# Four graph layers on one core: linear scores by one projection, the update gate from the reset gate's sum, a precomputed second hop, tanh for sigmoid, roots on GpSimd

## Chip, cores, metric

One core of a Trainium2 chip. Times are device microseconds of one execution. PE is TensorE (matmul), PEld its weight loads, DVE is VectorE, ACT is ScalarE, POOL is GpSimd. All executions quoted are in the fast state; repeats of one kernel agree within about 0.3%, once 0.4%.

## The reference, cut to what matters

x is [64, 256, 128] in fp32, adj is [256, 256]. Four layers, each added to its input after a layernorm and a relu:

```python
# layer 0, five steps                      # in_matrix = out_matrix = adj
u3 = h @ u3_w.T + u3_b
z = sigmoid(av @ w3_w.T + w3_b + u3)
r = sigmoid(av @ w4_w.T + w4_b + u3)
hv = tanh(av @ w5_w.T + w5_b + (r * h @ u5_w.T + u5_b))
h = (1.0 - z) * h + z * hv
# layer 1: hops x1 = A x0 and 2 A x1 - x0, concatenated, @ Theta1 + bias, relu
# layer 2: ((adj + I) h) W + bias, rows divided by their norm
# layer 3
pre = s1[:, :, None, :] + s2[:, None, :, :] + b_lin          # [b, i, j, 256]
h = where(pre >= 0, pre, 0.2 * pre)
attn = softmax(einsum('bije,e->bij', h, a) + adj, axis=2)
out = sigmoid(attn @ x)
```

## The kernel before

The batches go through in 32 pairs. Layer 3's scores are most of the work. For each row i of the 256, a relu of s2 plus row i's scalar is made on VectorE (two of three tiles) or ScalarE (every third), and TensorE reduces it over its 128 partitions with a stationary operand 32 columns wide. Four such matmuls use the four column groups of the array:

```python
for r in range(32):                       # one slot: rows r, 32+r, 64+r, 96+r of a row block
    for k in range(NE):                   # NE = 2 tiles a slot
        rl = relu_pool.tile([P, 4, NB, N], F32, name="rl")
        ...                               # 8 relus of 128x256, on VectorE or on ScalarE
        # four column groups of the array, which run side by side
        for g in range(4):
            nc.tensor.matmul(flat[g * 32:(g + 1) * 32, :], win[:, k, 31 - r:63 - r],
                             rl[:, g].rearrange("p b n -> p (b n)"), start=False, ...)
    background()                          # one stage of the next pair's layers 0 to 3, one of a softmax
```

I call the four matmuls of a tile a **quad**. The background of a gate step:

```python
pr = project([(w4t, mT), (u3t, hT)], "pr")       # two 128x512 products into one PSUM bank
pz = project([(w3t, mT), (u3t, hT)], "pz")
nc.scalar.activation(r, pr, AF.Sigmoid, bias=br, scale=1.0)
nc.scalar.activation(z, pz, AF.Sigmoid, bias=bz, scale=1.0)
nc.vector.tensor_mul(rh, r, hT)
yield
pv = project([(w5t, mT), (u5t, rh)], "pv")
```

The layernorm takes its root on ScalarE (`Sqrt`) and its reciprocal on VectorE. When the kernel is built, the framework's scheduler fixes the order of the instructions on each engine.

## Time and profile before

| | before |
|---|---|
| time | 7427.95 us, median of 3 (7426.46 to 7433.29) |
| TensorE busy | 7242 us (98%), ends modelled |
| VectorE busy | 6814 us (92%) |
| ScalarE busy | 5601 us (75%), of it 366 us of table loads |
| GpSimd busy | 0.7 us |

The prediction shows the main lines. One more view belongs beside it: the chain of work that ended last, in order of time, over one gate step of the kernel before. Columns: start in us, length in us, engine, tile, line, and the records. An fp32 matmul shows as two records.

```profile
3147.80 1.72 PE pz L212 x4
3149.51 1.85 PE pe L421 x16
3151.37 1.91 PE pv L212 x4
3153.28 3.57 PE pe L421 x32
3156.85 0.59 PE pt L197 x4
3157.44 1.85 PE pe L421 x16
3159.29 1.92 PE pm L205 x8
```

### The profile page before, as it was taken

Reading aid. Unit: us, or ns where it says so; the run is one execution under the profiler, and the core shown is the slowest. Engines: PE = TensorE matmul, PEld = TensorE weight load, DVE = VectorE, ACT = ScalarE, POOL = GpSimd, SP = SyncE. Lnnn points to the kernel's source line nnn. Section 1 sums busy time; section 2 is a strip of 40 time slices with the busy share of each in tenths; the row PEclk is TensorE's granted clock in tenths of the full one; section 3 lists DMA queues with packets and bytes.
Section 4 is the critical chain, followed back from the end, with each engine's and each line's share of the span. In section 5 each row is a group of like instructions: output and inputs, shape, how many; then the busy total and the mean of one; then the engine's idle time right before and its main releaser. Section 6 shows DMA issues by size and latency. Waiting matters only on the chain.

```text
span 7427.2 us, 120750 instructions
## 1 busy us (share of the span) xinstructions
PE 7242.1 (98%) x40713; PEld 2490.1 (34%) x40713; DVE 6813.8 (92%) x25298; ACT 5601.2 (75%) x12837; POOL 0.7 (0%) x6
## 2 busy tenths in 40 slices
PE   6999999999999999999999999999999999999999
PEld 3333333333333333333333333333333333333333
DVE  4998999999999999998999999999989999999999
ACT  3777777778777777777777777777877777777777
POOL 0000000000000000000000000000000000000000
PEclk8999999999999999999999999999999999999999
DMA  0000000000000000000000000000000000000000
GB/s 13 3 4 4 3 2 3 4 4 3 2 4 3 4 3 2 4 3 4 4 3 3 3 4 4 3 2 4 3 4 3 2 4 3 4 2 2 2 2 3
DMA packets 38816, 25.83 MB, mean 3 GB/s; under 512 B 3504, under 2 KB 38192, under 8 KB 38192
## 3 DMA queue, kind: packets, MB, share of 16 engines
q1 hardware_dynamic: 35088, 17.05, 0.8%
q8 instruction: 319, 5.23, 0.3%
q14 instruction: 305, 2.50, 0.1%
q10 hardware_dynamic: 3104, 1.05, 0.1%
HBM read 9.70 MB, written 8.39 MB: 2 GB/s over the span
## 4 chain that ended last, share of the span: by engine, by line
PE 87%; DVE 12%; ACT 1%; issue 0%; DMA 0%; SPq 0%; ACTq 0%; DVEq 0%
PE pe L421 58%; PE pm L205 7%; DVE rl L417 6%; PE pr L212 4%; PE pz L212 4%; PE pv L212 4%; PE pe L403 2%; PE pe L399 2%; PE pt L197 2%; DVE h L180 1%; PE po L222 1%; PE po L381 1%; PE pa L212 1%; PE pb L212 1%; DVE stats L173 1%; PE pt L189 1%
## 5 line engine op out<-in xcount | busy, mean ns | idle before, releaser
L417 DVE TENSOR_SCALAR rl<-s,s 128x256 f32<-128x256 f32 x21848 | 5868.7, 347 | 46.8 <-PE pe L421 44.5
L421 PE MATMUL pe<-rl,win 128*32 128x512 f32 x32768 | 5102.9, 599 | 93.4 <-DVE rl L417 93.4
L415 ACT ACTIVATE rl<-s,s 128x256 f32<-128x256 f32 x10920 | 4531.2, 497 | 399.6 <-PE pe L421 394.5
L421 PEld LDWEIGHTS pe<-rl,win 128*32 128x32 f32 x32768 | 1295.7, 109 | 3162.2 <-DVE rl L417 1569.0
L205 PE MATMUL pm<-adj_t,h 128*128 128x256 f32 x1280 | 336.0, 400 | 2.8 <-ACT h L274 2.8
L258 DVE TENSOR_TENSOR rh<-r,hT 128x512 f32<-128x512 f32 x160 | 109.8, 686 | 237.9 <-ACT r L254 237.3
L205 PEld LDWEIGHTS pm<-adj_t,h 128*128 128x128 f32 x1280 | 232.4, 195 | 166.3 <-issue 78.0
L249 ACT COPY mT<-pm 128x512 f32<-128x512 f32 x160 | 93.7, 586 | 155.3 <-PE pm L205 154.3
L254 ACT ACTIVATE r<-pr,gate_b 128x512 f32<-128x512 f32 x160 | 109.9, 687 | 114.5 <-PE pr L212 114.5
L369 ACT ACTIVATE sc<-sc,nmx 128x256 f32<-128x256 f32 x128 | 64.5, 504 | 157.3 <-DVE nmx L365 156.8
L212 PE MATMUL pr<-mT,w4t 128*128 128x512 f32 x320 | 178.9, 641 | 3.5 <-ACT mT L249 3.5
L212 PE MATMUL pv<-mT,w5t 128*128 128x512 f32 x320 | 179.5, 643 | 0.0
L403 PE MATMUL pe<-a_lin,s 128*128 128x256 f32 x512 | 168.6, 419 | 0.0
L212 PE MATMUL pr<-hT,u3t 128*128 128x512 f32 x320 | 167.3, 604 | 0.0
L212 PE MATMUL pz<-mT,w3t 128*128 128x512 f32 x320 | 165.9, 600 | 0.0
L212 PE MATMUL pv<-rh,u5t 128*128 128x512 f32 x320 | 164.5, 595 | 0.0
L262 ACT ACTIVATE hv<-pv,gate_b 128x512 f32<-128x512 f32 x160 | 108.7, 680 | 73.1 <-PE pv L212 73.0
L212 PE MATMUL pz<-hT,u3t 128*128 128x512 f32 x320 | 163.4, 592 | 0.0
L256 ACT ACTIVATE z<-pz,gate_b 128x512 f32<-128x512 f32 x160 | 109.3, 683 | 64.8 <-PE pz L212 64.8
L265 DVE TENSOR_TENSOR hv<-hv,hT 128x512 f32<-128x512 f32 x160 | 109.7, 686 | 37.7 <-ACT hv L262 36.3
L403 PEld LDWEIGHTS pe<-a_lin,s 128*128 128x128 f32 x512 | 80.9, 188 | 181.4 <-issue 179.8
L399 PE MATMUL pe<-s,a_lin 128*128 128x512 f32 x256 | 141.1, 640 | 0.0
(108 smaller groups left out, 3577.9 us busy)
## 6 DMA issues: line engine op xcount, KB each, us to landing
xin<-in_x_dram SPq DMA_DIRECT2D x64, 128.0 KB, 2.2
out_dram<-o SPq DMA_DIRECT2D x64, 128.0 KB, 1.8
w_raw<-in_L_gnn_w_w_dram ACTq DMA_DIRECT2D x3, 128.0 KB, 2.6
th_raw<-in_L_gnn_Theta_dram ACTq DMA_DIRECT2D x1, 320.0 KB, 3.4
adj_n<-in_adj_dram SPq DMA_DIRECT2D x1, 256.0 KB, 4.7
w_raw<-in_L_gnn_u_w_dram ACTq DMA_DIRECT2D x2, 64.0 KB, 2.6
bias<-in_L_gnn_bias_dram ACTq DMA_DIRECT2D x2, 64.0 KB, 3.5
w<-in_L_gnn_weight_dram ACTq DMA_DIRECT2D x1, 64.0 KB, 3.1
```

What stands on the lines that cost most here:

```text
L197: nc.tensor.transpose(pt[:, b, c, :], ht[:, b, c * P:(c + 1) * P], ident)
L205: nc.tensor.matmul(pm[:, b, :], h[:, b, c, :], a[:, c, :], start=(c == 0), stop=(c == NC - 1))
L212: nc.tensor.matmul(pp.rearrange("p b n -> p (b n)"), w, t.rearrange("p b n -> p (b n)"), start=(k == 0), stop=(k == len(pairs) - 1))
L254: nc.scalar.activation(r, pr, AF.Sigmoid, bias=br, scale=1.0)
L256: nc.scalar.activation(z, pz, AF.Sigmoid, bias=bz, scale=1.0)
L258: nc.vector.tensor_mul(rh, r, hT)
L265: nc.vector.tensor_sub(hv, hv, hT)
L399: nc.tensor.matmul(flat, a_lin[:, k, :P], s2[k].rearrange("p b n -> p (b n)"), start=(k == 0), stop=False, skip_group_check=True)
L403: nc.tensor.matmul(pe[:, b, :], s1[k][:, b, ic * P:(ic + 1) * P], a_lin[:, k, :], start=False, stop=False, skip_group_check=True)
L415: nc.scalar.activation(rl[:, g, b, :], s2[k][:, b, :], AF.Relu, bias=sc, scale=1.0)
L417: nc.vector.tensor_scalar(rl[:, g, b, :], s2[k][:, b, :], sc, 0.0, op0=OP.add, op1=OP.max)
L421: nc.tensor.matmul(flat[g * 32:(g + 1) * 32, :], win[:, k, 31 - r:63 - r], rl[:, g].rearrange("p b n -> p (b n)"), start=False, stop=(r == ...
```

## The change

It aims to take work off TensorE and ScalarE. Row i's own part of the linear scores is constant along j and cancels in the softmax; the other part is one projection of the layer's input. The update gate's sum is the reset gate's sum plus a difference of weights, so its product is added to the same PSUM bank after the reset gate has been read. The second hop uses a precomputed 2AA. Sigmoid becomes 0.5 + 0.5 tanh(x/2), and roots become a power on GpSimd, so that ScalarE needs one table. The core of the diff, with cuts marked:

```diff
+        nc.gpsimd.tensor_scalar(var, mv[:, :, 1], LN_EPS, None, op0=OP.add)
+        nc.gpsimd.tensor_tensor(rstd, var, neg_half, op=OP.pow)
-        nc.scalar.activation(std, mv[:, :, 1], AF.Sqrt, bias=eps_t, scale=1.0)
-        nc.vector.reciprocal(rstd, std)
 ...
             pr = project([(w4t, mT), (u3t, hT)], "pr")
-            pz = project([(w3t, mT), (u3t, hT)], "pz")
-            nc.scalar.activation(r, pr, AF.Sigmoid, bias=br, scale=1.0)
+            nc.scalar.activation(r, pr, AF.Tanh, bias=br, scale=0.5)
+            nc.tensor.matmul(pr.rearrange("p b n -> p (b n)"), w34t, mT.rearrange("p b n -> p (b n)"),
+                             start=False, stop=True, skip_group_check=True)
-            nc.scalar.activation(z, pz, AF.Sigmoid, bias=bz, scale=1.0)
+            nc.scalar.activation(z, pr, AF.Tanh, bias=bz, scale=0.5)
 ...
-        pt = to_token(c1T, "pt")
-        c1 = tok("c1")
-        nc.scalar.copy(c1, pt)
-        yield
-        pm = mix_nodes(c1, adj_n, "pm")
+        pm = mix_nodes(h, adj_2, "pm")
 ...  (y: four additions of the bias become one with a broadcast operand)
         norm_relu(x3, h3)
+        nc.gpsimd.tensor_scalar(x3, x3, 0.5, None, op0=OP.add)
 ...
-            for k in range(NE):
-                nc.tensor.matmul(flat, a_lin[:, k, :P], s2[k]..., start=(k == 0), ...)
-            for b in range(NB):
-                for k in range(NE):
-                    nc.tensor.matmul(pe[:, b, :], s1[k][:, b, ...], a_lin[:, k, :], ...)
+            nc.tensor.matmul(flat, lin_w, hT.rearrange("p b n -> p (b n)"), start=True, ...)
```

More of the change, by code (lines that the diff above doesn't have):

```diff
@@ L88 @@
     make_identity(nc, ident)
-    eps_t = const.tile([P, 1], F32, name="eps_t")
-    nc.vector.memset(eps_t, LN_EPS)
+    neg_half = const.tile([P, NB * NC], F32, name="neg_half")
+    nc.vector.memset(neg_half, -0.5)
     adj_n = const.tile([P, NC, N], F32, name="adj_n")
@@ L118, in load_transposed @@
         return t
-    w3t = load_transposed(w3_w, "w3t")
     u3t = load_transposed(u3_w, "u3t")
     w4t = load_transposed(w4_w, "w4t")
+    w34t = load_transposed(w3_w, "w34t")
+    nc.vector.tensor_sub(w34t, w34t, w4t)
     w5t = load_transposed(w5_w, "w5t")
     u5t = load_transposed(u5_w, "u5t")
+    nc.vector.tensor_scalar(u5t, u5t, 0.5, None, op0=OP.mult)
+    adj_2 = const.tile([P, NC, N], F32, name="adj_2")
+    for c in range(NC):
+        pq = bank([P, N], "pq")
+        for k in range(NC):
+            nc.tensor.matmul(pq, adj_t[:, k, c * P:(c + 1) * P], adj_n[:, k, :], start=(k == 0), stop=(k == NC - 1))
+        nc.vector.tensor_scalar(adj_2[:, c, :], pq, 2.0, None, op0=OP.mult)
     braw = const.tile([P, 5], F32, name="braw")
@@ L132 @@
     nc.vector.tensor_add(gate_b[:, 2:3], braw[:, 2:3], braw[:, 4:5])
+    nc.vector.tensor_scalar(gate_b[:, 0:2], gate_b[:, 0:2], 0.5, None, op0=OP.mult)
     bz, br, bh = gate_b[:, 0:1], gate_b[:, 1:2], gate_b[:, 2:3]
@@ L137 @@
     th = const.tile([P, 3, D], F32, name="th")
-    nc.vector.tensor_copy(th[:, 0, :], th_raw[:, 0, :])
     nc.vector.tensor_add(th[:, 1:3, :], th_raw[:, 1:3, :], th_raw[:, 3:5, :])
+    nc.vector.tensor_sub(th[:, 0, :], th_raw[:, 0, :], th[:, 2, :])
     w2 = const.tile([P, D], F32, name="w2")
@@ L158 @@
     nc.vector.memset(win, 0.0)
-    a_lin = const.tile([P, NE, N], F32, name="a_lin")
+    a_lin = const.tile([P, NE, P], F32, name="a_lin")
     nc.vector.memset(a_lin, ALPHA)
@@ L163 @@
         nc.vector.tensor_scalar(a_lin[:, k, :], a_lin[:, k, :], acol[:, k:k + 1], None, op0=OP.mult)
+    pl = bank([P, P], "pl")
+    for k in range(NE):
+        nc.tensor.matmul(pl, adj_n[:, k, P:2 * P], a_lin[:, k, :], start=(k == 0), stop=(k == NE - 1))
+    lin_w = const.tile([P, P], F32, name="lin_w")
+    nc.vector.tensor_copy(lin_w, pl)
     def norm_relu(src, h):
@@ L174, in norm_relu @@
             nc.vector.bn_aggr(mv[:, k, :], stats[:, k, :])
-        std = work.tile([P, NB * NC], F32, name="std")
-        nc.scalar.activation(std, mv[:, :, 1], AF.Sqrt, bias=eps_t, scale=1.0)
+        var = work.tile([P, NB * NC], F32, name="var")
+        nc.gpsimd.tensor_scalar(var, mv[:, :, 1], LN_EPS, None, op0=OP.add)
         rstd = work.tile([P, NB * NC], F32, name="rstd")
-        nc.vector.reciprocal(rstd, std)
+        nc.gpsimd.tensor_tensor(rstd, var, neg_half, op=OP.pow)
         for k in range(NB * NC):
@@ L251, in front @@
             pr = project([(w4t, mT), (u3t, hT)], "pr")
-            pz = project([(w3t, mT), (u3t, hT)], "pz")
             r = feat("r")
-            nc.scalar.activation(r, pr, AF.Sigmoid, bias=br, scale=1.0)
+            nc.scalar.activation(r, pr, AF.Tanh, bias=br, scale=0.5)
+            nc.tensor.matmul(pr.rearrange("p b n -> p (b n)"), w34t, mT.rearrange("p b n -> p (b n)"),
+                             start=False, stop=True, skip_group_check=True)
             z = feat("z")
-            nc.scalar.activation(z, pz, AF.Sigmoid, bias=bz, scale=1.0)
+            nc.scalar.activation(z, pr, AF.Tanh, bias=bz, scale=0.5)
             rh = feat("rh")
-            nc.vector.tensor_mul(rh, r, hT)
+            nc.vector.scalar_tensor_tensor(rh, r, 1.0, hT, op0=OP.add, op1=OP.mult)
             yield
@@ L265, in front @@
             nc.vector.tensor_sub(hv, hv, hT)
-            nc.vector.tensor_mul(hv, hv, z)
+            nc.vector.scalar_tensor_tensor(hv, z, 1.0, hv, op0=OP.add, op1=OP.mult)
             hT_new = feat("hT")
-            nc.vector.tensor_add(hT_new, hT, hv)
+            nc.vector.scalar_tensor_tensor(hT_new, hv, 0.5, hT, op0=OP.mult, op1=OP.add)
             hT = hT_new
@@ L291, in front @@
         yield
-        pt = to_token(c1T, "pt")
-        c1 = tok("c1")
-        nc.scalar.copy(c1, pt)
-        yield
-        pm = mix_nodes(c1, adj_n, "pm")
+        pm = mix_nodes(h, adj_2, "pm")
         c2T = feat("c2T")
-        nc.vector.scalar_tensor_tensor(c2T, pm, 2.0, hT, op0=OP.mult, op1=OP.subtract)
+        nc.scalar.copy(c2T, pm)
         yield
@@ L301, in front @@
         y = tok("y")
-        for k in range(NB * NC):
-            b, c = divmod(k, NC)
-            nc.vector.tensor_add(y[:, b, c, :], po[:, b, c, :], bias1)
+        nc.vector.tensor_add(y.rearrange("p b c d -> p (b c) d"), po.rearrange("p b c d -> p (b c) d"),
+                             bias1.unsqueeze(1).to_broadcast([P, NB * NC, D]))
         x2 = tok("x2")
@@ L318, in front @@
         y = tok("y")
-        for k in range(NB * NC):
-            b, c = divmod(k, NC)
-            nc.vector.tensor_add(y[:, b, c, :], po[:, b, c, :], bias2)
+        nc.vector.tensor_add(y.rearrange("p b c d -> p (b c) d"), po.rearrange("p b c d -> p (b c) d"),
+                             bias2.unsqueeze(1).to_broadcast([P, NB * NC, D]))
         yield
@@ L327, in front @@
         nc.vector.tensor_scalar(nrm, nrm, NORM_EPS * NORM_EPS, None, op0=OP.max)
-        nc.scalar.activation(nrm, nrm, AF.Sqrt)
         rn = work.tile([P, NB, NC], F32, name="rn")
-        nc.vector.reciprocal(rn, nrm)
+        nc.gpsimd.tensor_tensor(rn.rearrange("p b c -> p (b c)"), nrm.rearrange("p b c -> p (b c)"), neg_half,
+                                op=OP.pow)
         x3 = tok("x3", bufs=3)
@@ L340, in front @@
         norm_relu(x3, h3)
+        nc.gpsimd.tensor_scalar(x3, x3, 0.5, None, op0=OP.add)
         yield
         pt = to_feature(h3, "pt")
-        hT = feat("hT")
+        hT = feat("hT3")
         nc.scalar.copy(hT, pt)
@@ L356, in front, with tail @@
             yield
-        READY[p] = (x3, h3, s1, s2)
-    def tail(p, ic, pe, x3, h3):
+        READY[p] = (x3, h3, hT, s1, s2)
+    def tail(p, ic, pe, xh, h3):
         t = work.tile([P, NB, N], F32, name="sc")
@@ L372, in tail @@
         nc.vector.reciprocal(rs, sums)
+        nc.vector.tensor_scalar(rs, rs, 0.5, None, op0=OP.mult)
         yield
@@ L384, in tail @@
         for b in range(NB):
-            nc.scalar.activation(o[:, b, :], po[:, b, :], AF.Sigmoid, scale=rs[:, b:b + 1])
-        nc.vector.tensor_add(o, o, x3[:, :, ic, :])
+            nc.scalar.activation(o[:, b, :], po[:, b, :], AF.Tanh, scale=rs[:, b:b + 1])
+        nc.vector.scalar_tensor_tensor(o, o, 0.5, xh[:, :, ic, :], op0=OP.mult, op1=OP.add)
         nc.sync.dma_start(out[p * NB:(p + 1) * NB, ic * P:(ic + 1) * P, :].rearrange("b p d -> p b d"), o)
@@ L392, in scores @@
     def scores(p, background):
-        x3, h3, s1, s2 = READY.pop(p)
+        x3, h3, hT, s1, s2 = READY.pop(p)
         for ic in range(NC):
@@ L397, in scores @@
             flat = pe.rearrange("p b n -> p (b n)")
-            for k in range(NE):
-                nc.tensor.matmul(flat, a_lin[:, k, :P], s2[k].rearrange("p b n -> p (b n)"),
-                                 start=(k == 0), stop=False, skip_group_check=True)
-            for b in range(NB):
-                for k in range(NE):
-                    nc.tensor.matmul(pe[:, b, :], s1[k][:, b, ic * P:(ic + 1) * P], a_lin[:, k, :],
-                                     start=False, stop=False, skip_group_check=True)
+            nc.tensor.matmul(flat, lin_w, hT.rearrange("p b n -> p (b n)"),
+                             start=True, stop=False, skip_group_check=True)
             for r in range(32):
```

## The prediction

> **What bounds the kernel now.** I read the page's parts 1 and 2 first, then its chain, its costliest groups, the waits, and last a table of busy time by stretch over one pair of batches. Busy shares and chain of the kernel before:
>
> ```profile
> PE 7242.1 (98%) x40713; PEld 2490.1 (34%) x40713; DVE 6813.8 (92%) x25298; ACT 5601.2 (75%) x12837; POOL 0.7 (0%) x6
> PE 87%; DVE 12%; ACT 1%; issue 0%; DMA 0%; SPq 0%; ACTq 0%; DVEq 0%
> L417 DVE TENSOR_SCALAR rl<-s,s 128x256 f32<-128x256 f32 x21848 | 5868.7, 347 | 46.8 <-PE pe L421 44.5
> L421 PE MATMUL pe<-rl,win 128*32 128x512 f32 x32768 | 5102.9, 599 | 93.4 <-DVE rl L417 93.4
> L415 ACT ACTIVATE rl<-s,s 128x256 f32<-128x256 f32 x10920 | 4531.2, 497 | 399.6 <-PE pe L421 394.5
> ```
>
> At first sight TensorE is the bound (98%, 87% of the chain). That is too simple, since matmul ends are modelled. In the chain, sixteen score matmuls take 1.85 us when TensorE is pressed, so the two tiles of one slot of 4 rows cost it 1.85 us. VectorE issues one relu in 0.264 us (69 in a row took 18.20 us in the timeline): with 2 of 3 tiles of 8 relus each, a slot costs it 2 x 2/3 x 8 x 0.264 = 2.81 us. So a slot without other work is VectorE's, and TensorE binds only where layers 0 to 3 of the next pair lie beside the scores. Two chain pieces (start, length, what) and one pair cut into stretches (PE, PEld, DVE, ACT, POOL busy) show this:
>
> ```profile
> 3057.22 53.43 PE pe L421 x326
> ...
> 3128.78 1.72 PE pr L212 x4
> 3130.50 1.72 PE pz L212 x4
> 3132.22 1.85 PE pe L421 x16
> ```
>
> ```profile
> 3110.00:3128.00 18.00, 18.00 (x78) 6.11 (x74) 15.60 (x64) 11.80 (x26) 0.00 (x0) 1.00 0.01 1
> 3128.00:3208.00 80.00, 80.00 (x483) 28.77 (x482) 75.48 (x261) 67.11 (x153) 0.00 (x0) 1.00 0.01 3
> 3208.00:3277.00 69.00, 65.26 (x374) 23.05 (x370) 64.72 (x252) 50.72 (x117) 0.00 (x0) 1.00 0.02 7
> 3277.00:3342.00 65.00, 65.00 (x370) 20.92 (x370) 65.00 (x253) 50.56 (x120) 0.00 (x0) 1.00 0.00 1
> ```
>
> A: tail of the pair before and start of the front (18 us). B: the five gate steps, 17.2 us each (80 us). C: layers 1 to 3 (69 us). D: scores alone (65 us). In A and B TensorE is full: a gate step's pieces in the chain, 5 x 1.85 + 1.93 (mix) + 1.92 + 1.72 + 1.91 (projections) + 0.6 (transposes), sum to 17.3. But VectorE has 15.6 + 75.5 = 91.1 of those 98 us. C is a chain of VectorE work (norms, y, x) with waits. D is VectorE's alone: it is busy 65.00 of 65, and the 53.43 us piece gives 1.31 us per tile where TensorE could do 0.93. **VectorE is the floor everywhere, TensorE lies 7% above it in 98 us of a pair.** What VectorE idles is, in the waits (total, times, longest):
>
> ```profile
> DVE rh L258 <- ACT r L254: 237.3, 51, 10.6
> DVE s L350 <- PE pa L212: 60.9, 54, 2.3
> DVE c2T L298 <- PE pm L205: 59.1, 21, 11.0
> DVE y L321 <- PE po L222: 50.2, 32, 5.5
> ```
>
> Of 7427 - 6814 = 613 us idle, the first front, which nothing overlaps, has some 100 (it ends near 133 us; its five rh waits alone are 45). About 500 us are left, 16 per pair. One pair takes (7427 - 137) / 32 = 228 us.
>
> **What the Trainium skill says.** "Trainium Kernel Development and Optimization", its opening words on reading a trace: matmul busy time is a bad metric, because matmuls are pipelined. The trace agrees: score matmuls last 599 ns but sixteen pass in 1.85 us. "ScalarE: Activation LUTs", sections "What ACT_TABLE_LOAD costs" and "Table sets": a switch of set is a 1283 ns load; exp and tanh share a set, sqrt and sigmoid sit in others. The trace agrees: loads of 1283 ns, 94 + 94 + 54 + 31 + 12 = 285 of them, 365.7 us. "SBUF — State Buffer", section "Who interferes with whom": a VectorE instruction that uses both its ports holds a port pair shared with GpSimd, and the other is blocked for the whole instruction. The relus move 256 elements in 264 ns; at the 0.96 GHz that "VectorE: DVE Perf Modes", section "Specifications", gives, one element a cycle would need 267 ns and any overhead on top, so they must run in a two-element mode and hold that pair. GpSimd does nothing in this trace (0.7 us), so no run here shows the collision yet.
>
> **The change part by part** (per pair; 32 pairs).
> 1. Linear scores. Per row block, out: two 128x512 products and four 128x256 ones; in: one 128x512. In the chain at 3110 us the old ones are 1.06 + 1.06 + 0.43 + 0.63 + 1.06 = 4.24 us, the new one 1.06: 3.2 us less for each of two blocks. One block's lie in A, where TensorE is full; the other's around 3045 to 3057, where VectorE was busy without a gap: hidden. Busy time: 141.1 + 168.6 less about 70 = 239 us.
> 2. Update gate. Two products become one that accumulates on the reset gate's sum: one product of two records less per step, 0.86 us in the chain (1.72 for four), 4.3 us per pair, all in B (163 us busy).
> 3. Hop. Four transposes (21.5 us over the run) and one copy go; the other copy moves c2T from VectorE (0.69) to ScalarE. One stage less in the front.
> 4. Tanh, power. All 285 loads but the first go: 366 us of ScalarE, plus 38 + 7 us of roots. ScalarE is never full (80 us of B hold 67), so I count almost nothing. VectorE loses its reciprocals, 4 x 0.17 + 0.17 = 0.86.
> 5. Broadcast bias: 0.88 becomes about 0.68, twice: 0.4. New on VectorE: two small scalings, 2 x 0.15 = 0.3. The fused forms of the gate arithmetic cost as the plain ones (691 against 686 ns).
> 6. GpSimd gets 9 small instructions for roots and one 128x512 addition.
>
> On the path: A + B lose 4.3 + 3.2 = 7.5 us of TensorE, but VectorE's 91.1 us stop the gain at 6.9; with two nearly full engines I expect 4.5. C loses 0.69 + 0.86 + 0.4 - 0.3 = 1.65 us of VectorE work and perhaps 1.3 of its 4.3 us idle: 3. D gains nothing. GpSimd takes back an estimated 2.5: ten instructions, each a hand-over that stops VectorE for about 0.25 us, taken from the trace's only GpSimd work (100 to 292 ns apiece). Sum 4.5 + 3 - 2.5 = 5.0 us; x 31 = 155, plus 7 in the first front (shorter hop, no loads): 162. **7428 - 162 = about 7265 us**, 2.2% less.
>
> **The rivals.** (a) Everything removed pays: 424 us of TensorE (239 + 163 + 22) make 7000. For it: TensorE's 87% of the chain. Against: D is VectorE's, and VectorE alone needs 6814 - 60 plus the first front's idle 100, about 6850. (b) GpSimd becomes the wait. Norm and root stand in the middle of VectorE's stream; before, only 8.6 us were lost to the root, because some seven relus were put between. If GpSimd is locked out by those very relus and starts only when VectorE stops, each of 128 norms exposes about 2 us and each of 32 roots 1.5: 300 us, which gives 7428 - 162 - 80 (the 2.5 already taken) + 300, about 7490. Nothing in the profile of before speaks against it. (c) TensorE must wait for the reset gate to be read before it adds the difference: 0.69 us of ScalarE plus hand-over, about 0.9, as much as the saved 0.86. Score matmuls put between would hide it; if they don't, B gains nothing and about 5 x 0.86 x 0.6 = 2.6 us per pair are lost again: 7345. (d) The rh wait has another cause than TensorE's load; then 3 us per pair stay: about 7360.
>
> **Range and chances.** Centre 7265; (a) half true pulls to 7080, (b) half true with (c) pushes to 7430. The 2% line is 7279, so faster and same are nearly even: 0.50 faster, 0.43 same, 0.07 slower.
>
> **What would show each step.** Table loads 285 to a few, and ScalarE near 5200 us with no gain of its own; VectorE's busy time near 6750 and still at 93%; TensorE below VectorE's share or its score matmuls now waiting for relus in B; a gate step below 17.2 us, not below 16.5; D's slots unchanged at 2.81 us; the rh wait per pair about halved. Wrong would be shown by a wait of h on GpSimd's rstd over 1 us each (b), by relus longer than 264 ns apart beside GpSimd work, or by TensorE idle before the difference product (c).

## The result, and the profile after

8363.73 us median (8362.24 to 8364.41) against 7428.31: ratio 1.126, 95% interval 1.1244 to 1.1276. The change is 12.6% slower. (A ratio is the mean time of one kernel's fast runs over that of the other's of the same rounds, so not quite the ratio of the quoted medians.)

Busy times, chain by engine, and the two groups of the score work, after:

```profile
PE 7986.9 (96%) x39637; PEld 2439.2 (29%) x39637; DVE 6825.9 (82%) x24984; ACT 5189.8 (62%) x12393; POOL 284.4 (3%) x326
PE 77%; DVE 19%; POOL 3%; issue 1%; ACT 0%; DMA 0%; ACTq 0%; SPq 0%; DVEq 0%
L434 PE MATMUL pe<-rl,win 128*32 128x512 f32 x32768 | 6068.1, 604 | 287.5 <-DVE rl L430 286.7
L430 DVE TENSOR_SCALAR rl<-s,s 128x256 f32<-128x256 f32 x21848 | 5878.9, 345 | 11.1 <-PE pe L434 9.8
```

TensorE has 1076 records fewer and is busy 745 us longer. The score matmuls are the same 32768 records with nearly the same mean duration (604 against 599 ns), yet together they occupy 6068 us instead of 5103, 965 us more. Records that used to lie beside each other no longer do. The chain over the same part of a gate step shows how:

```profile
3014.43 1.00 PE pe L434 x8
...
3019.51 1.06 PE pr L232 x2
3020.56 0.98 PE pe L434 x2
3021.54 1.06 PE pr L232 x2
3022.59 0.98 PE pe L434 x2
3023.57 1.06 PE pr L274 x2
3024.63 1.85 PE pe L434 x14
3026.47 1.91 PE pv L232 x4
```

One single score matmul (x2) now stands between two 128-column products, and takes 0.98 us: as long as a whole quad (x8, 1.00 us). Seven matmuls (x14) take 1.85 us, as long as eight do. And each product split off by itself costs 1.06 us where a closed block of two costs 1.72 to 1.91. A gate step takes 20 to 22 us (pr to pr, median 21.9) instead of 17.2. The scores alone, without background, keep their pace: one piece of this chain is 64.16 us for 245 relus, 0.262 us each.

What VectorE waited for, after (total, times, longest):

```profile
DVE rh L279 <- ACT r L273: 630.6, 160, 8.5
DVE hv L286 <- ACT hv L283: 191.5, 160, 2.1
DVE y L335 <- PE po L242: 162.0, 32, 7.7
DVE h L200 <- POOL rstd L198: 154.6, 127, 2.4
DVE x L349 <- POOL rn L344: 28.9, 32, 1.1
```

The wait of rh, 237 us before, is 631: its producer sits behind a TensorE that is now slower (in e1 below, with TensorE's order restored, it is 47). The last two lines are new: 183 us of waiting for GpSimd's roots.

### The profile page after: what moved, and what is told of

The parts are those of the page before. It is cut to its first block, busy times and chain, and to the rows that moved or that the text cites. A ratio compares the mean times of both kernels' runs of the same rounds, so it can differ in the third digit from the quotient of the medians.

```text
span 8362.6 us, 117949 instructions
## 1 busy us (share of the span) xinstructions
PE 7986.9 (96%) x39637; PEld 2439.2 (29%) x39637; DVE 6825.9 (82%) x24984; ACT 5189.8 (62%) x12393; POOL 284.4 (3%) x326
## 4 chain that ended last, share of the span: by engine, by line
PE 77%; DVE 19%; POOL 3%; issue 1%; ACT 0%; DMA 0%; ACTq 0%; SPq 0%; DVEq 0%
PE pe L434 53%; DVE rl L430 13%; PE pm L225 7%; PE pr L232 4%; PE pv L232 4%; PE pr L274 2%; PE pt L217 2%; DVE h L200 2%; PE po L242 2%; POOL rstd L198 2%; DVE stats L193 1%; PE pa L232 1%; PE pt L209 1%; POOL var L196 1%; PE pb L232 1%; PE po L399 1%
## 5 line engine op out<-in xcount | busy, mean ns | idle before, releaser
L434 PE MATMUL pe<-rl,win 128*32 128x512 f32 x32768 | 6068.1, 604 | 287.5 <-DVE rl L430 286.7
L434 PEld LDWEIGHTS pe<-rl,win 128*32 128x32 f32 x32768 | 1448.5, 109 | 3820.9 <-DVE rl L430 2248.2
L279 DVE SCALAR_TENSOR_TENSOR rh<-r,hT 128x512 f32<-128x512 f32 x160 | 110.7, 692 | 630.6 <-ACT r L273 630.6
L225 PE MATMUL pm<-adj_t,h 128*128 128x256 f32 x1280 | 415.0, 425 | 2.8 <-ACT h L295 2.8
L196 POOL TENSOR_SCALAR var<-mv 128x4 f32<-128x4 f32 x128 | 58.1, 454 | 7232.8 <-DVE mv L194 7232.8
L295 ACT COPY h<-pt 128x512 f32<-128x512 f32 x128 | 75.2, 588 | 275.8 <-PE pt L217 275.8
L200 DVE TENSOR_SCALAR h<-x,mv,rstd 128x128 f32<-128x128 f32 x384 | 107.0, 342 | 115.1 <-POOL rstd L198 115.1
L307 ACT COPY hT<-pt 128x512 f32<-128x512 f32 x32 | 18.7, 586 | 271.2 <-PE pt L209 271.2
L274 PE MATMUL pr<-mT,w34t 128*128 128x512 f32 x320 | 180.1, 645 | 0.0
L379 DVE TENSOR_TENSOR sc<-pe,adj_n 128x256 f32<-128x256 f32 x128 | 49.7, 415 | 157.0 <-PE pe L434 157.0
L360 ACT COPY hT<-pt 128x512 f32<-128x512 f32 x32 | 18.7, 586 | 254.6 <-PE pt L209 254.6
```

The costliest lines, as they stand in the source:

```text
L196: nc.gpsimd.tensor_scalar(var, mv[:, :, 1], LN_EPS, None, op0=OP.add)
L200: nc.vector.tensor_scalar(hh[:, k, :], s[:, k, :], mv[:, k, 0:1], rstd[:, k:k + 1], op0=OP.subtract, op1=OP.mult)
L225: nc.tensor.matmul(pm[:, b, :], h[:, b, c, :], a[:, c, :], start=(c == 0), stop=(c == NC - 1))
L274: nc.tensor.matmul(pr.rearrange("p b n -> p (b n)"), w34t, mT.rearrange("p b n -> p (b n)"), start=False, stop=True, skip_group_check=True)
L279: nc.vector.scalar_tensor_tensor(rh, r, 1.0, hT, op0=OP.add, op1=OP.mult)
```

## The experiments

**A count.** From the order of instructions in each built program, or of the records in its trace, one can count how the score matmuls are parted. A run is an unbroken row of score matmuls between other matmuls; I charge it as many **passes** as its fullest column group has matmuls (four or fewer neighbours of a quad: one pass). The lengths above fit: x2, x8 take one pass of about 0.98 us, x14 and x16 two, 1.85 us. Counting a run's matmuls over four, rounded up, gives the same numbers in every kernel here. All kernels have 16384 score matmuls, at best 4096 passes.

| TensorE order free | runs | passes | us |
|---|---|---|---|
| before | 1566 | 4539 | 7428 |
| changed | 2193 | 5093 | 8364 |
| gate part alone (e3) | 2064 | 4977 | 7956 |
| changed without gate (e11) | 1509 | 4513 | 7652 |

Built and counted but not run: linear scores alone 4422 passes, hop alone 4477, tanh alone 4530, bias alone 4559, roots alone 4680. The gate is the part that scatters the quads most (438 passes more); the roots come next (141).

**Pinning TensorE.** In most runs every TensorE instruction is tied behind the one emitted before it:

```diff
+    def pe_matmul(*args, **kw):
+        return tc.keep_in_program_order(nc.tensor.matmul(*args, **kw))
+    def pe_transpose(*args, **kw):
+        return tc.keep_in_program_order(nc.tensor.transpose(*args, **kw))
-  nc.tensor.matmul(...)   nc.tensor.transpose(...)      (everywhere)
+  pe_matmul(...)          pe_transpose(...)
```

The other engines stay free, and their order may shift a little with it. In those traces all matmuls carry the helper's line.

Theory 1: parted quads are the loss. Rival 2: it is GpSimd, which stalls VectorE. Rival 3: it is TensorE's wait until the reset gate is read.

### e1: the changed kernel, pinned

> The changed kernel, with every TensorE instruction kept in the order in which the kernel's text emits it, so that the four column-group score matmuls of a tile are never parted by other matmuls. Counted in the program, the runs of score matmuls need (a run of n needs n/4, rounded up, passes of about 0.93 us) 4539 passes in the kernel before, 5093 in the changed one, 4096 here. Theory 1 (parted quads): the loss is gone, 7250 us (7000 to 7450), score matmuls' busy time back near 5000 us. Rival 2 (GpSimd's roots stall VectorE): still over 8100. Rival 3 (TensorE waits for the reset gate to be read): 8300 or more, since the program order puts that product right behind the gate.

7417.78 us, ratio 0.9987 (0.997 to 1.0003): 946 us less than the free changed kernel, with the same arithmetic. Rivals 2 and 3 fall as explanations of the main loss. It lies 168 us above the expected centre of 7250, though inside the range, so something else still eats the savings. Two groups of its TensorE:

```profile
L64 PE MATMUL pe<-rl,win 128*32 128x512 f32 x32768 | 5113.1, 606 | 220.1 <-DVE rl L437 218.1
L64 PE MATMUL pr<-mT,w34t 128*128 128x512 f32 x320 | 181.0, 648 | 124.5 <-ACT r L280 124.5
```

Score matmuls are back from 6068 to 5113 us, and now TensorE waits 218 us for relus and 124.5 us for the reset gate.

### e2: the kernel before, pinned

> The kernel before with the same pinning of TensorE's order. Theory 1: 443 passes fewer, but many of them lie where VectorE is the bound, so 7300 us (7150 to 7430). Rivals 2 and 3 have nothing to say of it: 7428.

7203.67 us, ratio 0.9697 (0.9682 to 0.9711). The kernel before had the same illness in a mild form; the gain is at the good end of what was expected. This is the base for the parts below. The pinned changed kernel is still 214 us slower than this one, so pinning does not account for the whole loss.

The theories leave out the granted clock of TensorE: 0.996 over the kernel before, 0.969 over e2. In e2's trace it is either full or half. Away from both ends (from 145 us to 30 us before the end), e2 has 386 us at half clock, in 63 stretches of 3.4 or 6.8 us, and in the 3.4 us before each of them TensorE was busy for 1.5 us at most. The kernel before and e3 have none there, the changed kernel has 184 us, e13 171, e9 253, e5 512 and e6 536. A product of eight records (pm) takes 3.75 us in such a stretch (e2 at 3150.64 us) and 1.94 at full clock (3133.08 us). So TensorE runs slower just after it has paused; what this costs was not separated.

### e3: the gate alone, order free

```diff
 ...  (w34t, the difference of the weights, is made once)
-            pz = project([(w3t, mT), (u3t, hT)], "pz")
             nc.scalar.activation(r, pr, AF.Sigmoid, bias=br, scale=1.0)
+            nc.tensor.matmul(pr..., w34t, mT..., start=False, stop=True, skip_group_check=True)
-            nc.scalar.activation(z, pz, AF.Sigmoid, bias=bz, scale=1.0)
+            nc.scalar.activation(z, pr, AF.Sigmoid, bias=bz, scale=1.0)
```

> The kernel before with the update gate's part alone (difference weights, product added to the reset gate's sum after its sigmoid, sigmoids and roots as before). Its program has 4977 passes in 2064 runs, against 4539 in 1566 before and 5093 in 2193 in the changed kernel. Theory 1: most of the loss is here, 7950 us (7800 to 8200). Rival 2: no loss, at most 7430. Rival 3: 7428 plus 160 waits of about 1 us at most, 7590.

7955.67 us, ratio 1.0708 (1.0692 to 1.0724), as theory 1 had it. One product less per step makes the kernel 527 us slower, without a single GpSimd instruction. Rival 3's 7590 is left far behind.

### e4: column groups of two tiles mixed

```diff
+                turns = ([(k, g) for g in range(4) for k in range(NE)] if mixed      # mixed: ic == 0 and 8 <= r < 16
+                         else [(k, g) for k in range(NE) for g in range(4)])
+                for k, g in turns:
 ...  (one score matmul; the relus of both tiles come first)
```

> The kernel before with TensorE pinned, but in 8 of the 32 slots of the first row block of each pair (those beside the gate steps; 256 slots in all) the eight score matmuls of a slot go column group by column group over both tiles, so that neighbours share a column group: 5 passes instead of 2 by the same counting, 768 more. Same results, same instructions. Theory 1: 768 x 0.93, where TensorE is full, about 700 us over the pinned kernel before (500 to 750). If column groups do not matter: no difference to it.

7202.34 us (2 runs), no different from e2. My expectation was wrong, and it corrected the count: neighbours on the same column group cost nothing as long as only score matmuls stand together. Sixteen records still took 1.85 to 1.87 us beside the gate steps. What a run costs is set by its fullest column group (two in both orders), not by who stands next to whom. The table above already counts in that way.

### e5 and e6: parting quads on purpose

e5 emits the background inside the second tile instead of behind it; e6 does so at another place in even slots only:

```diff
e5:
+                        if g == 1 and k == NE - 1:
+                            background()
-                background()
e6:
+                        if k == NE - 1 and g == (0 if r % 2 == 0 else 3):
+                            background()
-                background()
```

> The kernel before with TensorE pinned (7204 us as run), but the background work of a slot is emitted between column groups 1 and 2 of the slot's second tile instead of behind it. Quads are now parted in every slot that has TensorE background, but a run of score matmuls still holds two of each column group: 1029 runs and 4160 passes against 998 and 4096, counting for each run the most matmuls on one column group. Passes theory: at most 64 x 0.93 = 60 us more, 7204 to 7265. If parting as such costs: each of some 1000 partings costs a piece of 0.5 us or more, over 7500.

> As the parted run before it, but the background is emitted behind column group 0 of the second tile in even slots and behind column group 3 (the usual place) in odd ones. 998 runs, as in the pinned kernel before, but 4470 passes: 374 more, since runs now hold 11 and 5 matmuls in turn (3 + 2 passes) where they held 8 and 8 (2 + 2). Passes theory: 374 x 0.93 = 348 us where TensorE is the bound, so 7204 + 200 to 350 = 7400 to 7550. Parting as such, or the number of runs: no more than the run before it. Neither: 7204.

e5: 7414.99 us, ratio 0.9982 (0.9965 to 0.9999), 211 us over e2 where at most 60 were expected. e6: 7591.95 us, ratio 1.0224 (1.0206 to 1.0243). Score matmuls in the pinned kernel before, in e5 and in e6, and one wait of e5:

```profile
L63 PE MATMUL pe<-rl,win 128*32 128x512 f32 x32768 | 4598.0, 607 | 14.4 <-DVE rl L424 8.4 <-ACT rl L422 5.0
```

```profile
L63 PE MATMUL pe<-rl,win 128*32 128x512 f32 x32768 | 4624.9, 613 | 0.9
PE pt L66 <- DVE hT L275: 146.6, 160, 3.1
```

```profile
L63 PE MATMUL pe<-rl,win 128*32 128x512 f32 x32768 | 4932.2, 617 | 0.9
```

With 64 passes more, e5's score matmuls take 27 us longer, within the 60 that the count allows; its loss is elsewhere. In a pinned order the background now stands a few matmuls earlier and TensorE stops for its input (hT: 146.6 us, in e2 29.1), and 126 us more than in e2 run at half clock. Between e5 and e6, with 998 instead of 1029 runs but 310 passes more, score matmuls take 307 us longer, 0.99 us a pass, and the kernel 177 us. So here passes are what the matmuls cost, not the number of partings. The 177 us are not a clean price in time: e6 also waits 68 us less for hT than e5 (79.0 us). Both moved the background, and e6 lies 42 us above its expected range. Nor is busy time a measure of passes between kernels that differ in more than order: at the same 4096 passes, score matmuls take 4598 us in e2 and 5113 in e1, where TensorE waits 218 us for relus instead of 8.

### e7: only the roots on GpSimd, pinned

> The kernel before with TensorE pinned and only the roots moved to GpSimd as power. In the changed kernel's waits VectorE idles 154.6 us before h on rstd and 28.9 us before x on rn, 183 us. If this is lost on the path: 7204 + 150 to 190 = 7350 to 7395. If other work takes the place of the idle time: under 7260.

7383.53 us, ratio 0.9938 (0.9923 to 0.9953): 180 us over e2, just the idle time. In the changed kernel's trace the three kinds of GpSimd instruction were:

```profile
L198 POOL TENSOR_TENSOR rstd<-var,neg_half 128x4 f32<-128x4 f32 x128 | 132.7, 1037 | 10.7
L356 POOL TENSOR_SCALAR x<-x 128x512 f32<-128x512 f32 x32 | 59.6, 1863 | 39.6 <-DVE h L200 38.4 <-DVE mv L194 1.2
L196 POOL TENSOR_SCALAR var<-mv 128x4 f32<-128x4 f32 x128 | 58.1, 454 | 7232.8 <-DVE mv L194 7232.8
```

A power of four elements takes 1.04 us, so a root takes 1.5 us in two instructions. The built program of the changed kernel puts two relus (0.53 us) between the last statistic and h in 123 of 128 norms; the kernel before mostly had three to twelve there. So about 1.2 us stand open each time.

GpSimd and VectorE also hinder each other. In the first front of the changed kernel (first line), where VectorE runs statistics and no relus, var takes 0.23 us; beside relus (second line; so in all 123 norms with relus there) about 0.45:

```profile
119.32 0.23 POOL L196 TENSOR_SCALAR var<-mv 128x4 f32<-128x4 f32 x1 [2.52 <-DVE mv L194]
```

```profile
3154.60 0.45 POOL L196 TENSOR_SCALAR var<-mv 128x4 f32<-128x4 f32 x1 [4.23 <-DVE mv L194]
```

The extra 0.22 us is near one relu (0.264 us), as if it waited for one and then got in; the relus beside it are not longer than elsewhere. So GpSimd is not locked out until VectorE stops.

### e8: only the gate, pinned

> The kernel before with TensorE pinned and only the update gate taken from the reset gate's sum. TensorE saves 0.86 us per step but must now stand still until the reset gate's sigmoid has read the sum: 0.69 us plus hand-over. If the wait equals the saving: 7204 plus or minus 60. If score matmuls would have hidden it (that is, no wait): 7204 minus 100. If the wait is longer, behind a burst of relus on ScalarE: 7204 + 100 to 400.

7243.65 us, ratio 0.9748 (0.9734 to 0.9763), 40 us over e2. The chain:

```profile
3107.04 1.93 PE pr L63 x4
3108.97 0.03 issue
3109.00 0.69 ACT r L261
3109.69 0.04 issue
3109.74 1.12 PE pr L63 x2
```

TensorE stands still for 0.77 us (125.9 us in 160 waits) to save 0.86. With the order kept, rival 3 is right as a mechanism and takes back the whole saving. Where the 40 us on top come from was not traced.

### e9 and e10: the rest, pinned

e9 is the change without the gate and without GpSimd's roots; e10 also leaves the sigmoids.

> TensorE pinned, with the linear scores, the hop, tanh and the broadcast bias of the change, but without its gate and with the roots as before. The pinned changed kernel took 7418; the pinned kernel before 7204, GpSimd's roots alone add 180 to it and the gate alone 40. If the parts add up, the rest is worth 7418 - 7424 = -6, so about 7198. If they pay for themselves as predicted in the first row block and in layers 1 to 3 (some 3 us per pair): 7110.

> As the run before it, with the sigmoids left as they were, so no scaling on VectorE and no addition of 0.5 on GpSimd, but with the table loads. If table loads are hidden and the extra small work is not: 20 to 60 us below the run before it. If table loads cost on the path: above it.

e9: 7112.23 us, ratio 0.9577 (0.9563 to 0.9592). e10: 7062.83 us, ratio 0.9507 (0.9493 to 0.9521). Linear scores, hop and bias are worth 7203.67 - 7062.83 = 141 us. Tanh without the roots costs 49; how they divide was not separated. ScalarE still has 292 table loads in e9 (roots and exp alternate; 307 in e10), VectorE has the scaling of rs, and the 0.5 is added on GpSimd beside relus, which are busy 27 us longer (5904.1 us against 5877.1). The longest relu is 708 ns in e9 (first line) and 393 in e10 (second line; minimum, median and maximum in ns stand after the count):

```profile
L429 DVE TENSOR_SCALAR rl<-s,s x21848: 308/348/708, 137.1 to 7102.5; 128x256 f32<-128x256 f32 x199
```

```profile
L425 DVE TENSOR_SCALAR rl<-s,s x21848: 308/348/393, 134.8 to 7050.3; 128x256 f32<-128x256 f32 x199
```

### e11: the changed kernel without the gate, order free

> The changed kernel without its gate part, TensorE not pinned: 4513 passes against 5093. Passes theory with GpSimd's roots: as many passes as the kernel before (4539), plus 180 us for the roots, 7550 (7450 to 7650). If the order is not the cause: near 8360.

7651.8 us, ratio 1.03 (1.0282 to 1.0317), 712 us below the changed kernel: the cross-check of e3 from the other side. It is 2 us above the range.

### e12: a version that beats both

e10 with a new division of relu tiles:

```diff
-                    on_act = turn[0] % 3 == 1
+                    on_act = turn[0] % 8 in (1, 4, 6)
```

> A candidate to beat both: TensorE pinned, linear scores, hop and broadcast bias, and ScalarE takes 3 of 8 relu tiles instead of 1 of 3. VectorE's relus fall from 5869 to about 5500 us, ScalarE's rise from 4531 to about 5100. If VectorE is the floor once TensorE's order is repaired: 6850 to 7050. If TensorE or ScalarE has become the bound: 7150 or more.

6979.95 us, ratio 0.9396 (0.9382 to 0.941), 6% under the kernel before, and correct. VectorE falls to 6441 us, ScalarE rises to 6092.

### e13 and e14: what was still missing

The parts of the pinned change add up to 7204 - 92 + 180 + 40 = 7332, but e1 took 7418. e13 is the pinned change without the gate; e14 is e1 with the gate's product and its tanh moved behind the next `yield`, ahead of pv.

> The changed kernel without its gate, TensorE pinned: linear scores, hop, tanh, bias and GpSimd's roots. Without the roots this took 7112. If the roots cost here what they cost alone (180): 7292. If roots and the other parts together cost more than apart (the 86 us that are missing): up to 7378. Below 7260 the roots would be partly hidden and the gate would cost the rest.

> The changed kernel, TensorE pinned, with the product that adds the update gate's difference and its tanh emitted one stage later, ahead of pv, so that TensorE need not stand still for the reset gate (160 waits, 124.5 us in the pinned changed kernel, 7418). If these waits are on the path: 7418 - 60 to 124. If VectorE and the roots bound it anyway: 7418.

e13: 7382.8 us, ratio 0.9934 (0.9917 to 0.995). The roots cost 7383 - 7112 = 271 us beside the other parts, not 180; the gate costs 35, nearly as alone (40). So the missing 86 us belong to the roots. VectorE's direct wait for them is the same 183 us in e13 as in the changed kernel, and TensorE's wait for relus is 218 us against 28 in e9. How the further 90 us come about I did not separate; time at half clock is not it, since e13 has less of it than e9. e14: 7316.22 us, ratio 0.9847 (0.9832 to 0.9862). With the product one stage later the 124.5 us of waiting are gone and the time falls by 102 us; against e13 the gate is now worth 67 us.

## Why the prediction was wrong

**The step that failed** is the silent premise of its part by part sums: that the matmuls that stay cost what they cost before. "One product of two records less per step, 0.86 us in the chain ..., 4.3 us per pair, all in B" and "A + B lose 4.3 + 3.2 = 7.5 us of TensorE" take the two tiles of a slot at a fixed 1.85 us. They cost that only as whole quads. The sign stood in the stretch at 3110 us of the kernel before, from which the prediction took the lengths of the linear products: at 3111.71 us one score matmul (x2) stands alone between two of them and takes 0.98 us. The changed program had 5093 passes instead of 4539, and 627 more runs; each parting also opens a new block of products (a lone product 1.06 us instead of its share of about 0.86 to 0.95). A gate step took 20 to 22 us, not "below 17.2". Pinning the order took 946 us from the changed kernel (e1) but also 224 from the kernel before (e2), so 722 of the 935 us lost belong to the order. The 214 us between the two pinned kernels do not: the roots cost 271 (e9 to e13), the gate 35 (e13 to e1), and the other parts gain 92 (e2 to e9). Against its pinned twin, a free kernel loses 224 us for 443 passes over 4096 (before), 269 for 417 (e11), 712 for 881 (e3) and 946 for 997 (changed). That is 0.5 to 0.95 us a pass: loss and passes go together roughly, but the count alone does not give the time.

**Rival (c)** named the right spot and misjudged it. "Score matmuls put between would hide it": they were put between, often one at a time (665 lone score matmuls against 256 before), and this order was most of the loss. Pinned, its own mechanism shows as predicted: 0.77 us of standing still per step (0.9 predicted), a saving of 0.86 eaten (e8).

**Rival (b)**, GpSimd, had its mechanism half right. VectorE did wait for GpSimd's roots: 154.6 us in 127 norms, 1.2 us each instead of the feared 2, and 0.9 instead of 1.5 for each of 32 roots. But GpSimd was not locked out by the relus; only two relus stood between, and a power lasts 1.04 us. That a relu blocks GpSimd, or GpSimd a relu, for a whole instruction shows only in part (see the last section). The term "GpSimd takes back an estimated 2.5" per pair was mis-sized: 180 / 32 = 5.6 us alone (e7), 271 / 32 = 8.5 us beside the rest (e13). Taking it from instructions that fill constants, 100 to 292 ns each, was the error.

**Right**: D's slots did not change. ScalarE came to 5190 us ("near 5200") with one table load. That VectorE is the floor fits the pinned kernels only: it is busy 95% of e2, and taking 343 us of work from it gains 83 us (e10 to e12). Linear scores, hop and bias gave 141 us, 4.4 per pair; by the prediction's own shares they were worth 1.9 in A and B (4.5 x 3.2 / 7.5) and up to 2.4 in C (0.69 + 0.4 + 1.3), so 4.3. The 1.3 was a guess and the base is the pinned kernel, so part of this agreement is luck. No run has one table load without GpSimd's roots, so whether the removed loads alone are worth anything stays open.

**Wrong besides**: the rh wait was to halve and rose from 237 to 631 us. VectorE was to be busy near 6750 us, still 93%, and was 6826, 82%. The range's ends, 7080 and 7430, do not follow from the sums shown: midway to (a)'s 7000 lies 7132, and midway to (b)'s 7490, with (c)'s 80 added, 7457.

**Not shown**: why the scheduler scatters quads with this gate. That the order does it is shown; its reason lies in the build, and a late product alone, order free, still counts 4939 passes (built, not run).

## What to carry to other kernels

When small matmuls share the array side by side, count them in the built order before and after a change: a product that is removed can let the scheduler put full-width matmuls between them, and one of four left alone costs as much as four. Price a change to an engine's order, not only its list of instructions; where the order matters, pin it, and place a product that must wait for another engine one stage later. Look at the granted clock of the pinned kernel too. And before moving a short dependent step to an idle engine, measure that engine's one instruction of that kind.

## What the Trainium skill lacked or had wrong

- "TensorEngine Tiling (Array Packing)", section "Key Properties", says that changing the tiling mode drains the TensorE. I overlooked it, and the trace agrees in kind: four records right behind other 128-column products take 1.72 us (pz before), behind score matmuls 1.91 (pv), and a lone product between score matmuls 1.06. The page gives no price: a lone 32-column fp32 score matmul took 0.98 us, a whole quad 1.00, and a pass more cost about 0.99 us of the score matmuls' busy time (e5 to e6).
- No page that I read says that the order of column groups within a run is free: eight matmuls ordered 0, 0, 1, 1, 2, 2, 3, 3 took 1.85 to 1.87 us, as in the usual order (e4).
- "GPSIMD Engine Reference", section "Performance versus the Vector engine", has no price for a power: 128x4 took 1037 ns. Its best case for 512 elements, a tight unrolled loop, is 769 ns; adding a scalar to 128x512 took 1863 ns in the mean (1736 at least).
- "SBUF — State Buffer", section "Who interferes with whom", says that whoever issues first holds the shared pair for its whole instruction and the other is fully blocked. The runs show less, as far as GpSimd's spans, which are rough, can tell: while one addition of 0.5 lasted 1.87 us (changed kernel) or 1.79 (e9), VectorE ran h and a relu at their usual 0.42 and 0.34 us, and just two relus took 0.70. This is so in 31 of 32 additions. The page does not say how a GpSimd instruction fares against VectorE instructions that follow one another: var took 0.23 us beside statistics and 0.45 beside relus.
- "ScalarE: Activation LUTs", section "What ACT_TABLE_LOAD costs", adds a drain of about 1380 ns to each load of 1283 ns. The load agrees, 1283 ns; the drain shows on neither side: in the kernel before, ScalarE idles 0.8 us in all before the 54 loads of the last sigmoid and 5.2 us in all between them and that sigmoid; the 94 loads before the exp have 1.7 us before them.
